# Grouping the count products of a graph kernel's sweep into runs of two and of four

## The chip, the core and the metric

The kernel runs on one core of one Trainium2 chip. Five engines of that core matter here, each working through its own list of instructions in order: TensorE (PE, matrix products; its weight loads are listed as PEld), VectorE (DVE), ScalarE (ACT), GpSimd (POOL, which here issues indirect DMAs) and SyncE (SP, which issues plain DMAs). Products are written to PSUM, eight banks of 2 KB for each of the 128 partitions; ACT and DVE read them there.

The metric is the device time of one launch in microseconds (us), lower is better. Three runs of the kernel before gave 1506.61 us as their median (1501.49 to 1509.82).

## What is computed

A graph layer over 6250 nodes with 200000 edges and 256 features, followed by a mixture of 64 experts and two normalisations. The edges come sorted by destination, and destinations crowd at low node numbers.

```python
deg_out = clip(segment_sum(ones, src), 1); deg_in = clip(segment_sum(ones, dst), 1)
h  = x * rsqrt(deg_out)[:, None]
m  = segment_sum(h[src], dst) * rsqrt(deg_in)[:, None]
x1 = m @ W_gc + b_gc + x @ W_res + b_res
core = top-2 of 64 experts on x1 (256 -> 512, gelu, -> 256)
y  = batch_norm(x1 + core) * gamma + beta
out = layer_norm(x + y)
```

The change concerns `segment_sum(h[src], dst)`, which the kernel does in a stage called the sweep.

## The kernel before, in words

The kernel first counts degrees, scales the rows and writes them to DRAM (`h_dram`) while keeping a copy in SBUF (`hrow`). Then comes the sweep, from about 171 to 906 us of the profile, and after it the routing, the experts and the normalisations.

**Two ways through the edges.** Edges are taken in groups of 128. The first 1118 groups, whose destinations lie close together, are *dense*: they are cut into 30 chunks (`DENSE`, numbered 0 to 29). A chunk covers a window of 128 destination nodes and consists of n parts; a part consists of k groups whose destinations fit into w columns. Chunks 0 to 4 have k = 4, 3, 2, 2, 2; from chunk 5 on k is 1, and (w, n) go from (4, 51) in chunk 5, (5, 50), (5, 46), (5, 42) in chunks 6 to 8 and (6, 39) to (6, 33) in chunks 9 to 12, over (7, 31) to (7, 27) in chunks 13 to 17 and (8, 26) to (8, 22) in chunks 18 to 23, to (9, 22) to (9, 20) in chunks 24 to 29. The remaining 445 groups are *gathered*: POOL fetches their source rows by an indirect DMA (L626) into a ring of eight tiles, and PE adds them to one PSUM bank `pg` (L631 and L632), 28 windows one after another.

**What one dense part costs.** `count` (L704) makes one product for each group, from two one-hot matrices in bf16, `lo` (128 source places) and `hotk` (49 source tiles times w columns): L712, 49·w columns wide, into a PSUM bank `pc`. So a product of chunk 14 is 343 columns wide. There are five banks `pc`. After the last group of a part ACT copies all but the first column of every source tile into the tile `counts` (L732, L729), and DVE adds the first column to what is there (L749). Both read the bank, so it comes free when both are done. The addition of part j isn't issued with part j: `carried(1)` (L745) leaves one part waiting at each call, so it is issued on DVE at the place of part j + 2.

**What makes the one-hots.** DVE makes `hotk` (L699) in cuts that hold two groups from w = 5 to w = 9, with four buffers: after the last product of a cut, the cut four further is issued, which waits on DVE until that product has read the buffer. `lo` (L287) is made once in eight groups. DVE also makes the one-hots `hot` of the gathered groups (L935, four groups at a time).

**What is multiplied.** `multiply(c, t)` (L755) multiplies the counts of chunk c by source tile t: two products of 258 and 256 columns in fp32r (L758, L759), t running over the 49 tiles of `hrow`. The sums of a chunk lie in one of two banks `sm`.

**What sets the order.** The generator `dense` (L879) writes the order out by hand, and all engines' lists follow it. For chunk c it walks over t = 0 to 48; ahead of `multiply(c, t)` it puts the parts of chunk c + 1 that fall on t, part j on t = 1 + 42·j // n. So the parts of one chunk are spread over the first 42 steps of the chunk before. Each item carries a weight in us, and a loop behind puts a gathered group between two items whenever the weights so far have passed the next group's due time. From t = 10 on, `x_step` (L853) puts in small steps that finish rows of an earlier window: on DVE L788, L792, L795, then L823, L828, L832, L835 and L836; on ACT a square root (L789) and a copy (L808); on PE transposes and gate products (L805, L814). When a gathered window is complete, PE adds an overlap product (L956), ACT copies `pg` out (L958), and the next window's first product waits for that copy, since there is one bank `pg`.

In the steps below, "chunk c" in connection with a time is the stretch in which chunk c is multiplied and chunk c + 1 is counted.

Of the kernel before, what the change touches and what calls it, by code (L numbers as in the profile page):

```python
# [161 lines left out]
def gnn_moe_kernel(ctx, tc, x_in, x_cols, src, dst, bases, nexts, firsts, parts, lasts, W_gc, b_gc, W_res, b_res, Wg, bg, w1, b1, w2, b2,  # L162
# [84 lines left out]
    with tc.tile_pool(name="edges", bufs=1) as ep, ExitStack() as later:  # L247
# [52 lines left out]
        with tc.tile_pool(name="late", bufs=1) as lp, tc.tile_pool(name="both", bufs=2) as bp, \  # L300
# [62 lines left out]
            for k, values in enumerate((LOW, HIGH)):  # L363
                c = 0
# [141 lines left out]
            for i in range(NGR // CG):  # L506
# [32 lines left out]
                for c in range(CG):  # L539
                    r = c % 2  # L540
# [19 lines left out]
                if i % 6 == 0 and 6 <= i <= 42:  # L560
                    r = i // 6 * 7
# [44 lines left out]
        with tc.tile_pool(name="xs", bufs=1) as xs, tc.tile_pool(name="hotg", bufs=2) as hg, \  # L606
# [12 lines left out]
            for i in range(NR):  # L619
                r = rp.tile([128, 2 * D + 2], F32R, name=f"r{i}")  # L620
# [29 lines left out]
            def halves(t):  # L650
                at = range(t - 1, min(t + 1, NS))
                for u in at:
                    S.activation(hrow[:, u, :D], f32(hrow[:, u, D:2 * D]), AF.Copy, scale=s_out[:, u:u + 1])
                for u in at:
                    V.scalar_tensor_tensor(hrow[:, u, D:2 * D], f32(hrow[:, u, D:2 * D]), s_out[:, u:u + 1],
                                           f32(hrow[:, u, :D]), op0=ALU.mult, op1=ALU.subtract)
                if t % 5 == 4 or t % 10 == 5:
                    n = 6 if t % 10 == 5 else 4
                    n -= max(t + 1 - NS, 0)
                    t0 = at[-1] + 1 - n  # L660
                    source_out(f32(hrow[:, t0:t0 + n, :2 * D]), h_dram, t0, n)
# [22 lines left out]
            def lo_of(q):  # L684

                if q * PAIRS < GD:
                    los[q] = hc.tile([128, PAIRS // 2, 128, 2], BF16, name="lo")
                    hot_pairs(los[q], lo_b, q * PAIRS, PAIRS, 128)

            def hot_of(q):  # L690

                if q >= len(cuts):
                    return
                a, b, w = cuts[q]
                e, m = a - a % 2, NS * w
                n = b + b % 2 - e
                hot = hc.tile([128, n * m], BF16, name="hotk", bufs=KB, padded_shape=[128, NS * LANES])
                hot = hot.rearrange("p (c j r) -> p c j r", j=m, r=2)
                V.tensor_tensor(hot, pairs(key, e, n, m), iota_h[:, None, :m, :].to_broadcast([128, n // 2, m, 2]),  # L699
                                ALU.is_equal)  # L700
                for g in range(a, b):
                    hots[g] = hot[:, (g - e) // 2, :, (g - e) % 2]

            def count(g):  # L704

                c, j, i = groups[g]
                g0, k, w, n = DENSE[c]
                if i == 0:
                    live["pc"] = ps_c.tile([128, 512], F32, name="pc")
                r = g % PAIRS  # L710
                pc = live["pc"][:, :NS * w]
                T.matmul(pc, los[g // PAIRS][:, r // 2, :, r % 2], hots.pop(g), start=(i == 0),  # L712
                         stop=(i == k - 1))
                if i == k - 1:
                    if j % 8 == 0:
                        _, live["at"] = nc.values_load_multi_w_load_instructions(
                            places[c:c + 1, j:j + 8], engines=(ACT_E, DVE_E), min_val=0, max_val=WIN - w,
                            skip_runtime_bounds_check_because="clipped to what the window leaves")
                    carried(1)
                    at, pc = live["at"][j % 8], pc.rearrange("p (t w) -> p t w", w=w)  # L720
                    if j == 0:
                        live["adds"], live["carry"], live["puts"] = [], [], []
                    if c == 0 and j == 0:
                        live["puts"].append(S.copy(counts[0][:, :, :w], pc).ins)
                    else:
                        if j == 0:
                            step = nc.values_load(step_i[0:1, c:c + 1], engines=(DVE_E,), min_val=0, max_val=WIN - 1,
                                                  skip_runtime_bounds_check_because="clipped to the window")
                            put = S.copy(counts[c % 2][:, :, 1:w], pc[:, :, 1:])  # L729
                            to, had = counts[c % 2][:, :, 0:1], counts[(c - 1) % 2][:, :, ds(step, 1)]  # L730
                        else:
                            put = S.copy(counts[c % 2][:, :, 1:][:, :, ds(at, w - 1)], pc[:, :, 1:])  # L732
                            to = had = counts[c % 2][:, :, ds(at, 1)]
                        for a in live["adds"]:
                            tc.declare_no_dep(put.ins, a, reason="other columns of the window")
                        live["carry"].append((to, pc[:, :, 0:1], had, j))
                        live["puts"].append(put.ins)
                if g % PAIRS == 1:
                    lo_of(g // PAIRS + 1)
                if g == cuts[cut_of[g]][1] - 1:  # L740
                    hot_of(cut_of[g] + KB)
                if i == k - 1 and j == n - 1:
                    carried(0)

            def carried(but):  # L745

                while len(live["carry"]) > but:
                    to, more, had, j = live["carry"].pop(0)
                    add = V.tensor_tensor(to, more, f32(had), ALU.add).ins  # L749
                    tc.add_manual_dep(add, live["puts"][j].name, SYNCED, reason="its bank, and the column of the part in front")  # L750
                    for a in live["puts"][j + 1:]:
                        tc.declare_no_dep(add, a, reason="columns behind it")
                    live["adds"].append(add)
# [125 lines left out]
            def dense():  # L879

                def of_one_hots(c):
                    g0, k, w, n = DENSE[c]
                    return n * (0.18 + k * (0.09 + 0.035 * w)) + 4.0

                lo_of(0)
                made_of = 1
                for q in range(KB):
                    hot_of(q)
                    halves(made_of)
                    made_of += 2  # L890
                S.activation(counts[0][:, 40:, :], iota_f[:, None, :].to_broadcast([128, NS - 40, WIN]), AF.Copy, scale=0.0)
                g, n = 0, DENSE[0][1] * DENSE[0][3]
                for g in range(n):
                    yield of_one_hots(0) / n, lambda g=g: count(g)
                    if g % 4 == 3:
                        yield 1.0, lambda t=made_of: halves(t)
                        made_of += 2
                for c in range(ND):
                    todo, us = {}, 0.0
                    if c < ND - 1:  # L900
                        g0, k, w, n = DENSE[c + 1]
                        us = max(0.021 + 0.0208 * w, (of_one_hots(c + 1) - 12.6) / (n * k),
                                 (n * (0.2 + w * 0.03) + 5.0 - 12.6) / (n * k))
                        for j in range(n):
                            todo.setdefault(1 + j * 42 // n, []).extend(range(g0 + j * k, g0 + j * k + k))
                    for t in range(NS):
                        for g in todo.get(t, []):
                            yield us, lambda g=g: count(g)
                        if c == 0 and t % 2 == 0 and made_of <= NS:
                            yield 1.0, lambda t=made_of: halves(t)  # L910
                            made_of += 2
                            if made_of > NS:
                                yield 0.0, lambda: first_rows()
                        if c == 0 and t == 45:
                            yield 0.0, lambda: left_edges()
                        yield 0.24, lambda c=c, t=t: multiply(c, t)
                        if 10 <= t < 46:
                            yield 0.04, lambda c=c, t=t: x_step(c, t)
# [44 lines left out]
            def first_rows():  # L963
                for n in range(NR):
                    fetch(ring[n], srcg[:, rows[n][1] - GD:rows[n][1] - GD + 1])
                hot_rows(0)

            now, n = 0.0, 0
# [155 lines left out]
    with tc.tile_pool(name="xw", bufs=1) as xw, tc.tile_pool(name="xl", bufs=3) as xl, \  # L1124
# [42 lines left out]
        with tc.manual_schedule():  # L1167
            sums = {}
            for t0 in range(ta, tb, 2):
                n = min(2, tb - t0)  # L1170
# [9 lines left out]
            for t0, z in sums.items():  # L1180
                n = min(2, tb - t0)
# [27 lines left out]
            for a, b in ((0, ta), (tb, NT)):  # L1209
                for t0 in range(a, b, 10):  # L1210
                    n = min(10, b - t0)
# [673 lines left out]
```

## Time and profile before

| | |
|---|---|
| median of three runs | 1506.61 us |
| the profiled execution | 1507.11 us |
| its span, first to last instruction | 1505.1 us |
| busy PE, DVE, ACT, POOL over the span | 90%, 75%, 51%, 53% |
| count products L712 | 1118, mean 304 ns |
| multiply products L758, L759 | 1470 each, mean 346 and 282 ns |
| copies out of `pc`, L732 | 879, mean 406 ns |
| additions of the first column, L749 | 908, mean 241 ns |
| one-hots L699 | 488, mean 507 ns |

A product's listed duration overlaps that of its neighbours, so the cost of one is read from the distance between starts. In rows of the timeline the columns are: start in us from the span's start, duration in us, engine, line, operation, what is written from what, shape, how many rows were merged (x2 is two instructions), and in brackets the idle time of the engine before it and what ended it.

### The profile page before, as it was taken

To read this page: it belongs to the slowest core of one execution; us is meant where nothing else is said; L and a number is where in the kernel's file an instruction comes from. 1 tells how busy PE (TensorE), PEld (TensorE's weight loads), DVE (VectorE), ACT (ScalarE), POOL (GpSimd) and SP (SyncE) were. 2 spreads that over 40 slices of the span, in tenths; PEclk is the share of its full clock that TensorE was granted. 3 is DMA by queue.
4 is the path that set the end of the run, shared out by engine and by line. 5 is a ranking of instruction groups with operands and counts; after the bars stand their busy time and mean duration, and the time that the engine had idled before them with its cause. 6 is when DMAs were issued, how large, how long until landed. Compare 5 with 4: busy or idle time off the path is not lost. (4 is left out here: it accounts for less than half of the span.)

```text
span 1505.1 us, 33098 instructions
## 1 busy us (share of the span) xinstructions
PE 1347.8 (90%) x9805; PEld 1127.7 (75%) x9805; DVE 1127.2 (75%) x3325; ACT 763.2 (51%) x1966; POOL 797.9 (53%) x897
## 2 busy tenths in 40 slices
PE   5999478988999999999999994699999999999783
PEld 3555266877888899999999993588788888788441
DVE  8999889988888888888777746745555655444587
ACT  4676544456666666665555533433343333333358
POOL 6000215777776677776666635256666667565100
PEclk8999789999999999999999996899999999999888
DMA  5899665778777778787777755669777788687645
GB/s 180 264 283 323 240 241 155 197 220 236 201 221 221 220 214 232 210 221 211 222 203 217 214 156 192 125 196 295 229 247 253 253 251 268 206 250 246 236 142 155
DMA packets 211234, 332.81 MB, mean 221 GB/s; under 512 B 27989, under 2 KB 142814, under 8 KB 211045
## 3 DMA queue, kind: packets, MB, share of 16 engines
q1 hardware_dynamic: 156035, 176.48, 37.5%
q0 software_dynamic: 47888, 146.88, 34.4%
q10 hardware_dynamic: 7122, 7.26, 1.7%
q8 instruction: 79, 1.29, 0.4%
q14 instruction: 110, 0.90, 0.2%
HBM read 250.92 MB, written 73.15 MB: 215 GB/s over the span
## 5 line engine op out<-in xcount | busy, mean ns | idle before, releaser
L626 POOL DMA_INDIRECT r<-h_dram,srcg x445 | 469.8, 1056 | 243.3 <-PE pc L712 80.2
L758 PE MATMUL sm<-hrow,counts 128*128 128x258 f32 x1470 | 487.0, 346 | 8.8 <-DVE counts L749 8.7
L732 ACT CAST counts<-pc 128x196 f32 (+7 forms) x879 | 356.9, 406 | 211.1 <-PE pc L712 175.4
L759 PE MATMUL sm<-hrow,counts 128*128 128x256 f32 x1470 | 394.5, 282 | 0.0
L712 PE MATMUL pc<-hotk,lo 128*128 128x245 bf16 (+7 forms) x1118 | 304.7, 304 | 42.5 <-DVE counts L749 20.3
L758 PEld LDWEIGHTS sm<-hrow,counts 128*128 128x128 f32 x1470 | 286.6, 195 | 27.4 <-issue 12.4
L699 DVE TENSOR_TENSOR hotk<-key,iota_h 128x784 bf16<-128x784 f16 (+4 forms) x488 | 247.6, 507 | 57.9 <-PE pc L712 55.8
L759 PEld LDWEIGHTS sm<-hrow,counts 128*128 128x128 f32 x1470 | 279.8, 190 | 1.3
L749 DVE TENSOR_TENSOR counts<-pc,counts 128x49 f32 x908 | 218.6, 241 | 48.3 <-ACT counts L732 10.3
L1523 ACT ACTIVATE hT<-ph,bc 128x112 f32<-128x112 f32 (+16 forms) x256 | 108.4, 428 | 265.4 <-PE ph L1521 255.1
L1521 PE MATMUL ph<-xgT,w1s 128*128 128x112 f32 (+17 forms) x1024 | 198.7, 340 | 0.4 <-DVE xgT L1506 0.4
L1521 PEld LDWEIGHTS ph<-xgT,w1s 128*128 128x128 f32 x1024 | 166.0, 192 | 20.5 <-issue 2.2
L1481 POOL DMA_INDIRECT y_dram<-ys,dest x124 | 120.7, 973 | 106.5 <-ACT ys L1575 68.9
L712 PEld LDWEIGHTS <-lo 128*128 128x128 bf16 x1118 | 99.5, 100 | 74.9 <-issue 17.1
L631 PE MATMUL pg<-r,hot 128*128 128x258 f32 x445 | 144.5, 325 | 2.9 <-DMA r<-h_dram,srcg 2.4
L1481 POOL DMA_INDIRECT xg<-x_dram,ids x124 | 119.0, 959 | 49.8 <-issue 15.2
L632 PE MATMUL pg<-r,hot 128*128 128x256 f32 x445 | 125.1, 281 | 0.0
L1537 PE MATMUL py<-w2s,hT 128*128 128x256 f32 (+4 forms) x440 | 105.2, 382 | 0.0
L470 PE MATMUL pr<-wcat,f 128*128 128x512 f32 x196 | 100.8, 638 | 0.8 <-DMA wcat<-in_L_gnn_W_res_dram 0.8
L1506 DVE TENSOR_SCALAR xgT<-pte,bsum 128x112 f32<-128x112 f32 (+14 forms) x128 | 48.7, 421 | 67.2 <-PE pte L1503 67.0
L287 DVE TENSOR_TENSOR lo<-lo_b,iota 128x1024 bf16<-128x1024 bf16 x140 | 96.0, 686 | 3.3 <-issue 2.9
L1559 PE MATMUL ph<-hT,w2s 128*128 128x208 f32 (+8 forms) x464 | 95.0, 358 | 0.0
(361 smaller groups left out, 1965.8 us busy)
## 6 DMA issues: line engine op xcount, KB each, us to landing
w1s<-in_L_gnn_w_dram SPq DMA_DIRECT2D x64, 512.0 KB
w2s<-in_L_gnn_w_dram SPq DMA_DIRECT2D x64, 512.0 KB
y_dram<-zeros SPq DMA_DIRECT2D x48, 256.0 KB
yr<-y_dram SPq DMA_DIRECT2D x10, 1024.0 KB
h_dram<-hrow SPq DMA_DIRECT2D x5, 1536.0 KB
r<-h_dram,srcg POOLq DMA_INDIRECT x445
f<-in_x_cols_dram SPq DMA_DIRECT2D x25, 256.0 KB
z_dram<-zeros ACTq DMA_DIRECT2D x7, 903.0 KB
```

The costliest lines, as they stand in the source:

```text
L626: G.indirect_dma_start(out=f32(r[:, :2 * D]), out_offset=None, in_=h_dram[:, :], in_offset=bass.IndirectOffsetOnAxis(ap=idx, axis=0))
L631: T.matmul(pg, hot, r[:, D:], start=first, stop=False)
L632: T.matmul(pg[:, :D], hot, r[:, :D], start=False, stop=last)
L699: V.tensor_tensor(hot, pairs(key, e, n, m), iota_h[:, None, :m, :].to_broadcast([128, n // 2, m, 2]), ALU.is_equal)
L712: T.matmul(pc, los[g // PAIRS][:, r // 2, :, r % 2], hots.pop(g), start=(i == 0), stop=(i == k - 1))
L732: put = S.copy(counts[c % 2][:, :, 1:][:, :, ds(at, w - 1)], pc[:, :, 1:])
L749: add = V.tensor_tensor(to, more, f32(had), ALU.add).ins
L758: T.matmul(sm, by, hrow[:, t, D:], start=(t == 0), stop=False)
L759: T.matmul(sm[:, :D], by, hrow[:, t, :D], start=False, stop=(t == NS - 1))
L1481: w = G.indirect_dma_start(**kw)
L1521: T.matmul(ph[:, :m], w1s[:, kk, c * 128:(c + 1) * 128], xgT[:, kk, :m], start=(kk == 0), stop=(kk == 1))
L1523: S.activation(hT[:, c, :m], ph[:, :m], AF.Gelu, bias=b1_e[:, c:c + 1])
```

## The change

From now on the unit that is put ahead of `multiply(c, t)` is not a group but all that falls on t, as one item; and where a part has one group (chunk 5 and later), parts are moved to the step of the first of two (while chunks 4 to 11 are multiplied, so parts of chunks 5 to 12) or of the first of four (while chunks 12 to 28 are multiplied, parts of chunks 13 to 29). Since a gathered group is only put between items, none can stand inside such a run any more; this holds for chunks 1 to 4 too, whose parts otherwise stay where they are. The weights add up to the same sum.

```diff
                         us = max(0.021 + 0.0208 * w, (of_one_hots(c + 1) - 12.6) / (n * k),
                                  (n * (0.2 + w * 0.03) + 5.0 - 12.6) / (n * k))
+                        at_once = 1 if k > 1 else 2 if c < 12 else 4
                         for j in range(n):
-                            todo.setdefault(1 + j * 42 // n, []).extend(range(g0 + j * k, g0 + j * k + k))
+                            todo.setdefault(1 + (j - j % at_once) * 42 // n, []).append(range(g0 + j * k, g0 + j * k + k))
                     for t in range(NS):
-                        for g in todo.get(t, []):
-                            yield us, lambda g=g: count(g)
+                        if t in todo:
+                            yield us * sum(len(r) for r in todo[t]), lambda t=t, todo=todo: [count(g) for r in todo[t] for g in r]
```

What this does to PE's list, at the start of chunk 13 (parts 0 to 3 of chunk 14; weight loads left out). Before:

```order
L759 MATMUL sm1_2856<-hrow_104,counts1_2821 128x256
...
L712 MATMUL pc_10016<-hotk_9913,lo_9868 128x343
L758 MATMUL sm1_2856<-hrow_104,counts1_2821 128x258
...
L712 MATMUL pc_10042<-hotk_9913,lo_9868 128x343
L631 MATMUL pg_9753<-r6_2849,hot_9872 128x258
L632 MATMUL pg_9753<-r6_2849,hot_9872 128x256
...
L712 MATMUL pc_10052<-hotk_9932,lo_9868 128x343
```

With the change:

```order
L759 MATMUL sm1_2856<-hrow_104,counts1_2821 128x256
...
L712 MATMUL pc_10016<-hotk_9913,lo_9864 128x343
...
L712 MATMUL pc_10040<-hotk_9913,lo_9864 128x343
...
L712 MATMUL pc_10045<-hotk_9923,lo_9864 128x343
...
L712 MATMUL pc_10049<-hotk_9923,lo_9864 128x343
L631 MATMUL pg_9761<-r6_2849,hot_9874 128x258
L632 MATMUL pg_9761<-r6_2849,hot_9874 128x256
```

Four count products, each into another bank, now follow one another. Until the next four, five pairs of L758 and L759 and two pairs of L631 and L632 stand there. Over chunks 4 to 11 the count products stand in 167 runs where they stood in 314, and over chunks 12 to 28 in 108 where they stood in 411.

DVE's list in chunk 13, from the additions of parts 4 and 5 of chunk 14 to that of part 6 (sequencer rows left out). Before:

```order
L749 TENSOR_TENSOR counts0_2820<-pc_10071,counts0_2820 128x49
...
L749 TENSOR_TENSOR counts0_2820<-pc_10079,counts0_2820 128x49
L287 TENSOR_TENSOR lo_10102<-lo_b_94,iota_2_73 128x1024
L699 TENSOR_TENSOR hotk_10104<-key_92,iota_h_85 128x686
L788 TENSOR_SCALAR s_in_10108<-z_9779 125x2
...
L749 TENSOR_TENSOR counts0_2820<-pc_10092,counts0_2820 128x49
```

With the change:

```order
L749 TENSOR_TENSOR counts0_2820<-pc_10071,counts0_2820 128x49
...
L749 TENSOR_TENSOR counts0_2820<-pc_10075,counts0_2820 128x49
L287 TENSOR_TENSOR lo_10089<-lo_b_94,iota_2_73 128x1024
L699 TENSOR_TENSOR hotk_10091<-key_92,iota_h_85 128x686
L936 TENSOR_TENSOR hot_10095<-keyg_93,iota_f_71 128x512
L788 TENSOR_SCALAR s_in_10108<-z_9783 125x2
...
L749 TENSOR_TENSOR counts0_2820<-pc_10081,counts0_2820 128x49
```

On DVE nearly the same instructions stand in nearly the same order (here one `hot` has moved behind the two additions). What differs is where on PE's side they belong: the last row, the addition of part 6, is issued at the place of part 8, which is now the first of the third run of four; part 11, the last of that run, is the one that takes the bank of part 6.

## The prediction

> **What bounds the kernel now.** I first read the page's slices (PE, then DVE, 37.6 us each), to see which engine is full where.
>
> ```profile
> span 1505.1 us, 33098 instructions
> PE   5999478988999999999999994699999999999783
> DVE  8999889988888888888777746745555655444587
> ```
>
> The sweep is slices 5 to 24. Both engines are full at first, and DVE's share falls while PE's stays. The windows cut the sweep finer: length, then busy time of PE, weight loads, DVE, ACT and POOL with their instructions, PE's clock, DMA share and GB/s. The stretches are chunks 4 to 7, 8 to 12, 13 to 17, 18 to 23, and 24 to 28.
>
> ```profile
> 323.40:434.70 111.30, 101.65 (x779) 89.26 (x779) 98.33 (x362) 70.19 (x205) 83.03 (x80) 1.00 0.78 220
> 434.70:555.30 120.60, 115.64 (x896) 105.79 (x897) 104.29 (x372) 75.83 (x193) 85.52 (x80) 1.00 0.79 220
> 555.30:661.90 106.60, 106.18 (x828) 99.41 (x827) 89.51 (x304) 66.89 (x155) 78.55 (x73) 1.00 0.78 219
> 661.90:788.30 126.40, 126.40 (x975) 119.62 (x974) 101.27 (x337) 75.90 (x164) 82.36 (x81) 1.00 0.75 213
> 788.30:890.20 101.90, 101.90 (x778) 96.47 (x778) 73.78 (x234) 58.71 (x118) 65.25 (x64) 1.00 0.75 211
> ```
>
> From 555 us on PE never stops (106.18 of 106.60, then all): there a saved product is saved time, and a stalled one is lost. Up to 555 us PE is open for 10 and 5 us and DVE is busy 88% and 86%; the two hold each other up. What PE waits for there is in the view of the additions L749 between 323 and 555 us (who waited, us, times); in the same view of 555 to 890 us PE's count products don't appear.
>
> ```profile
>   PE pc L712: 10.4, 27
> ```
>
> So banks come free just in time before 555 us, and early enough after it.
>
> **What a run saves on PE.** The timeline of PE gives a count product alone (294 columns, then 196), and in a run of two and of four.
>
> ```profile
> 450.32 0.28 PE L759 MATMUL sm<-hrow,counts 128*128 128x256 f32 x1
> 450.44 0.30 PE L712 MATMUL pc<-hotk,lo 128*128 128x294 bf16 x1
> 450.48 0.39 PE L758 MATMUL sm<-hrow,counts 128*128 128x258 f32 x1
> 450.70 0.28 PE L759 MATMUL sm<-hrow,counts 128*128 128x256 f32 x1
> ...
> 309.97 0.28 PE L758 MATMUL sm<-hrow,counts 128*128 128x258 f32 x1
> 310.09 0.28 PE L759 MATMUL sm<-hrow,counts 128*128 128x256 f32 x1
> 310.21 0.44 PE L712 MATMUL pc<-hotk,lo 128*128 128x294 bf16 x2
> 310.38 0.38 PE L758 MATMUL sm<-hrow,counts 128*128 128x258 f32 x1
> 310.60 0.28 PE L759 MATMUL sm<-hrow,counts 128*128 128x256 f32 x1
> ...
> 330.78 0.28 PE L759 MATMUL sm<-hrow,counts 128*128 128x256 f32 x1
> 330.90 0.26 PE L712 MATMUL pc<-hotk,lo 128*128 128x196 bf16 x1
> 330.94 0.36 PE L758 MATMUL sm<-hrow,counts 128*128 128x258 f32 x1
> 331.14 0.28 PE L759 MATMUL sm<-hrow,counts 128*128 128x256 f32 x1
> ...
> 219.28 0.28 PE L759 MATMUL sm<-hrow,counts 128*128 128x256 f32 x1
> 219.40 0.52 PE L712 MATMUL pc<-hotk,lo 128*128 128x196 bf16 x4
> 219.70 0.37 PE L758 MATMUL sm<-hrow,counts 128*128 128x258 f32 x1
> 219.91 0.28 PE L759 MATMUL sm<-hrow,counts 128*128 128x256 f32 x1
> ```
>
> One fp32r product costs 0.12 us (309.97 to 310.09). From 450.32 to 450.70 lie two of them and one count product: 0.38 - 0.24 = 0.14 us for it. From 310.09 to 310.60 lie two and two: 0.51 - 0.24 = 0.27, so the second cost 0.13. A product that is taken into a run saves 0.01 us at 294 columns. At 196 columns it is 0.36 - 0.24 = 0.12 alone and 0.63 - 0.24 = 0.39 for four, 0.03 us saved for each of three. No run of 343 columns or more exists in this trace. I take 0.01 for all, since 294 is the nearer width, with 0 and 0.03 as ends. Runs fall from 314 to 167 over chunks 4 to 11 and from 411 to 108 over chunks 12 to 28: 147 · 0.01 = 1.5 us and 303 · 0.01 = 3.0 us, together -4.5 us (0 to -13.5).
>
> [...]
>
> **What a run costs in banks.** There are five banks `pc`. Part j + 5 takes the bank of part j, which needs the copy on ACT and the addition on DVE, and that addition is issued at the place of part j + 2. With single parts DVE may lag behind PE by three parts before PE stalls. In a run of four the addition of part 6 is issued at the first (part 8) and the bank is wanted by the last (part 11), three products later. At 343 columns a product in a run is about 0.157 us (estimate: 0.135 · 343/294), so the allowed lag shrinks to 0.47 us. How far DVE lags in the present kernel, at part 6 of chunk 14: PE starts part 8 and part 11, DVE makes the addition.
>
> ```profile
> 560.20 0.33 PE L712 MATMUL pc<-hotk,lo 128*128 128x343 bf16 x1
> ...
> 562.14 0.33 PE L712 MATMUL pc<-hotk,lo 128*128 128x343 bf16 x1
> ```
>
> ```profile
> 561.51 0.23 DVE L749 TENSOR_TENSOR counts<-pc,counts 128x49 f32 x1
> ```
>
> It ends at 561.74, 1.54 us after its place and 0.40 before its bank is wanted. With only 0.47 us of room it would have held PE for 1.07 us. That is the bad end. But between runs PE now spends longer on other products, and DVE has only additions and one-hots of the last run to do. So I walk one period, with DVE's costs as distances between starts and ACT's from a string of copies.
>
> ```profile
> 565.35 0.68 DVE L935 TENSOR_TENSOR hot<-keyg,iota_f 128x512 fp32r<-128x512 f16 x1
> 565.95 0.28 DVE L636 TENSOR_SCALAR overg<-iota_f,shift 128x128 f32<-128x128 f32 x1
> ...
> 566.30 0.68 DVE L287 TENSOR_TENSOR lo<-lo_b,iota 128x1024 bf16<-128x1024 bf16 x1
> 566.90 0.51 DVE L699 TENSOR_TENSOR hotk<-key,iota_h 128x686 bf16<-128x686 f16 x1
> 567.33 0.59 DVE L749 TENSOR_TENSOR counts<-pc,counts 128x49 f32 x2
> 567.82 0.51 DVE L699 TENSOR_TENSOR hotk<-key,iota_h 128x686 bf16<-128x686 f16 x1
> ```
>
> ```profile
> 561.63 0.20 ACT L789 ACTIVATE s_in<-s_in 125x2 f32<-125x2 f32 x1 [1.04 <-DVE s_in L788]
> 562.40 2.18 ACT L732 CAST counts<-pc 128x294 f32 x5 [0.56 <-PE sm L759]
> ```
>
> A `hot` costs 0.60, a `lo` 0.60, a `hotk` 0.43, two additions 0.49, a copy 0.44 us. Second run of chunk 13 in the changed order, T its first product. `hotk` must wait for the second product, which starts 0.157 in and takes 0.33: about T + 0.5, done T + 0.95. The additions of parts 4 and 5 need the copies, which begin once the first product is out (about T + 0.4) and end about T + 0.85 and T + 1.3, so they are done at T + 1.5. Then `lo` to T + 2.1, `hotk` to T + 2.5, `hot` to T + 3.1, L788 to T + 3.2, and the addition of part 6 ends at T + 3.4. PE's period is four products (0.63) and seven pairs (7 · 0.24 = 1.68), 2.3 us, and the last of the third run wants the bank at T + 2.3 + 0.47 = T + 2.8. PE stalls 0.6 to 0.7 us. The same walk over the other runs of that chunk gives 0.4 and 0.2 us, then nothing; 1.3 us. ACT adds to this where its square root stands ahead of the copies and waits for L788 (1.04 us above).
>
> From such walks I estimate 1.2, 1.3, 0.8, 0.6 and 0.3 us for chunks 12 to 16 (7 columns), together 4.2; about 0.4 us each for chunks 17 to 22, whose period is 2.9 us for hardly more DVE work, 2.4; and 0.3 for the rest. Sum +6.9 us; the ends are 0 and 23 us (a quarter of a microsecond at each of 91 runs that are not first in their chunk, a quarter of the 1.07 us).
>
> Named behind the stalled product on PE: every multiply and gathered product, since PE works in order; POOL's next fetch waits for them but has a ring of eight.
>
> A second, smaller wait is ACT's: where a gathered window closes just behind a run, its copy out of `pg` stands behind four copies (4 · 0.44 = 1.8 us), and the next gathered product is due 0.5 to 1.0 us of PE time after the overlap product. In the changed order this is so in chunks 13, 14, 18, 19 and 22. Some 0.3 us each, +1.5 us (0 to 4).
>
> In chunks 4 to 11 the second of two products comes a multiply (0.24 us) or more earlier than it did, while its bank comes when DVE gets there. If the 27 waits became 54 of 0.3 us more, it would be +8 us; if twos let DVE run more evenly, at most the 10.4 us go. I take +2, because DVE's work is the same and sets that stretch. Chunks 0 to 3 I leave at 0: only gathered products move, and DVE is full there.
>
> The Trainium skill (Perfetto Trace Analysis, section Optimizing Tensor Performance, Matmuls) asks that independent products rotate through banks so that the emptying of one overlaps the next's products. That speaks against a run that takes four of five banks at once. The trace's 10.4 us of bank waits before 555 us agree with it.
>
> **The sum.** -4.5 + 6.9 + 1.5 + 2 = +5.9 us. The profiled execution had 1507.1 us (2.0 of it outside the span), half a microsecond over the median, so 1513 us.
>
> **The rivals.**
>
> *PE gains and nothing waits.* For it: the view of one-hots L699 between 555 and 890 us shows DVE idle for PE's count products:
>
> ```profile
>   PE pc L712: 46.9, 74
> ```
>
> so DVE has room, 14% of 335 us, and might be ahead at each run's start. Against it is the lag of 1.54 us above, in a stretch where that room exists too. Then -4.5 us, 1502.6, or at 0.03 us a product -13.5, 1493.6. [...]
>
> *Every run waits.* The mechanism of the walk, at all 91 runs: from the point where DVE's lag at the start of a run passes 0.47 us as a rule, PE pays what DVE owes. +23 - 3 = +20, 1527. For it: the lag of part 6. Against: at 9 columns the period grows to some 3.4 us and DVE's work doesn't follow (73.78 of 101.90 busy).
>
> *The first stretch eases.* Twos make DVE's waits for ACT rarer and PE's bank waits before 555 us go: up to -10.4 there, against the +8.4 behind; about 1503. For it: DVE is idle 13 us in 323 to 434 while PE waits too. Against: no instruction of DVE gets cheaper.
>
> That the change doesn't do what it says is excluded by the listed rows: the runs stand in PE's list.
>
> **How the numbers follow.** Forecast as walked (1507 to 1519) 0.46; nothing waits 0.22; every run waits 0.19; the first stretch eases 0.13. About 0.5%, 7.5 us, is what a measurement can tell here: faster is under 1499.1, slower over 1514.1. Faster: half of the first rival, some of the third, 0.14. Slower: all of "every run waits" and nearly half of the forecast, 0.40. Within: 0.46. The range runs from 1498 to 1528, with the likeliest case's own 1507 to 1519 in it.
>
> **What would show it.** In the changed profile, the windows behind 555 us should show PE open for some us in chunks 12 to 16, ended by DVE's L749, and hardly any in chunks 23 to 28. Starts inside a run should be about 0.155, 0.175 and 0.20 us apart at 343, 392 and 441 columns. PE's waits for `pc` should lie on the last product of a run. The forecast is wrong if PE stays closed there, if starts in a run are as far apart as a product alone costs, or if the first stretch moves by more than 5 us.

## The result and the profile after

| | before | after |
|---|---|---|
| median, same chip | 1506.98 us (6 runs, 1501.49 to 1509.82) | 1520.64 us (6 runs, 1519.38 to 1524.48) |
| the profiled execution | 1507.11 us | 1520.51 us |
| its span | 1505.1 us | 1518.8 us |

After / before is 1.0095, with a 95% interval of 1.0078 to 1.0113: the change costs 13.7 us, where +5.9 was predicted. The range held it; the loss was more than twice the sum.

The page's slices of the kernel after show PE's slices 25 and 26 fuller, since the sweep ends later; the loss itself is too small to be seen in them.

```profile
span 1518.8 us, 33067 instructions
PE   5999488988999999999999995789999999999783
DVE  9999889988888887877777755845555655454597
```

The windows of the same five stretches as in the prediction (chunks 4 to 7, 8 to 12, 13 to 17, 18 to 23, 24 to 28; length, then busy time of PE, weight loads, DVE, ACT and POOL, PE's clock, DMA share and GB/s), each cut up to 2.4 us later than at the same events:

```profile
326.30:437.70 111.40, 100.51 (x781) 88.01 (x780) 98.50 (x364) 70.38 (x205) 82.30 (x79) 1.00 0.77 218
437.70:560.80 123.10, 116.37 (x900) 104.10 (x899) 105.36 (x376) 76.51 (x194) 86.30 (x81) 1.00 0.77 215
560.80:673.00 112.20, 105.37 (x819) 95.22 (x818) 89.69 (x298) 66.26 (x154) 71.62 (x73) 1.00 0.73 206
673.00:805.40 132.40, 127.90 (x978) 115.27 (x977) 104.17 (x339) 76.43 (x165) 82.87 (x81) 1.00 0.74 203
805.40:909.50 104.10, 102.39 (x786) 92.56 (x785) 73.12 (x231) 58.07 (x117) 63.93 (x63) 1.00 0.73 205
```

The first stretch is about as long as before (111.40 against 111.30 us). From 560.8 us on PE is open for 6.8, 4.5 and 1.7 us, where before it stood open for 0.4, 0 and 0. The clock was 1.00 in all of them, before and after.

For a finer account I cut at the copies of the finished sums (L762). Up to the end of chunk 3 the kernel is 1.8 us longer, chunks 4 to 11 are 0.4 longer (209.0 to 209.4), chunks 12 to 28 are 14.7 longer (358.4 to 373.1), and what lies behind, where no list changed, is 3.2 shorter; the sum is the 13.7 of the spans. I have no cause for the first and the last of these; the experiments below show that both vary by more from one execution to the next.

What PE waited for in chunks 12 to 28 (532 to 890 us before, 534 to 907 after), by the view of waits; the columns are who waited for what, us in total, times, and the longest. Before:

```profile
PE sm L758 <- DVE counts L749: 1.0, 2, 0.7
```

After:

```profile
PE pc L712 <- DVE counts L749: 10.6, 19, 1.1
PE pg L631 <- issue: 1.5, 1, 1.5
PE pg L631 <- ACT resg L959: 1.2, 3, 0.7
PE sm L758 <- DVE counts L749: 1.0, 1, 1.0
```

The count products wait for the additions of DVE, which before they never did here. This view counts from the listed end of the product in front, and that overlaps; by distances between starts (what is over 0.152, 0.173 and 0.198 us at 343, 392 and 441 columns) the loss is 14.8 us in 25 of 97 runs of four, all of it on the fourth product. The other waits of PE in the stretch come to 5.3 us by distances, and before there were 1.6 in all. So 20.1 - 1.6 = 18.5 us of waits came and the stretch grew by 14.7, which leaves about 3.8 us for what the runs saved.

In chunks 4 to 11 the same rows are, before and then after:

```profile
PE pc L712 <- DVE counts L749: 10.4, 27, 1.2
PE sm L758 <- DVE counts L749: 2.6, 6, 0.7
```

```profile
PE pc L712 <- DVE counts L749: 11.6, 27, 1.6
PE sm L758 <- DVE counts L749: 1.1, 4, 0.4
```

They moved between products and hardly changed in sum.

**One stall, read through.** Chunk 28 multiplies and chunk 29 is counted. The timeline of PE has the third run of four (parts 8 to 11):

```profile
892.72 0.28 PE L759 MATMUL sm<-hrow,counts 128*128 128x256 f32 x1
892.84 0.76 PE L712 MATMUL pc<-hotk,lo 128*128 128x441 bf16 x3
894.46 0.37 PE L712 MATMUL pc<-hotk,lo 128*128 128x441 bf16 x1 [0.86 <-DVE counts L749]
```

The x3 end at 893.60, the last of them began at 893.60 - 0.37 = 893.23, so the step inside the run is 0.39 / 2 = 0.195 us; the fourth should have begun at 893.43 and began at 894.46. It needs the bank of part 6. DVE between the additions of parts 4 and 5 and those of parts 6 and 7:

```profile
890.78 0.62 DVE L749 TENSOR_TENSOR counts<-pc,counts 128x49 f32 x2
891.31 0.69 DVE L287 TENSOR_TENSOR lo<-lo_b,iota 128x1024 bf16<-128x1024 bf16 x1
891.91 0.61 DVE L699 TENSOR_TENSOR hotk<-key,iota_h 128x882 bf16<-128x882 f16 x1
892.44 0.37 DVE L788 TENSOR_SCALAR s_in<-z 125x2 f32<-125x2 f32 x1
892.51 0.69 DVE L936 TENSOR_TENSOR hot<-keyg,iota_f 128x512 fp32r<-128x512 f16 x1
893.11 0.16 DVE L792 RECIPROCAL s_in<-s_in 125x2 f32<-125x2 f32 x1
893.30 0.88 DVE L795 SCALAR_TENSOR_TENSOR xr<-z,s_in,xr 125x256 f32<-125x256 f32 x2
894.16 0.52 DVE L749 TENSOR_TENSOR counts<-pc,counts 128x49 f32 x2
```

DVE works without a pause from 890.78 on. The copy of part 6, the third of four that ACT makes from 890.10 to 892.17, ended at about 891.65, so its addition is 2.5 us late. It is issued at the place of part 8, behind one-hots and the four steps that finish rows of an earlier window (L788, L792 and two L795; I call them the row steps). PE's period between the two runs (889.64 to 892.84, 3.2 us) is no longer than that list (890.78 to 894.16, 3.4 us).

The row steps run once in a stretch, from t = 10 on, and only in 15 of the 17 chunks 12 to 28, since chunks 16 and 24 have no rows to finish. In all 15 the third run of four stalls on its last product (part 11: 15 stalls, 10.8 of the 14.8 us); in chunks 16 and 24 it doesn't. Two more things stand at that place. L792 needs the square root that ACT makes of what L788 wrote, and now often nothing lies between them on DVE. The view of the line L792 in chunks 12 to 28 has this wait, and before it had none:

```profile
  ACT s_in L789: 3.0, 10
```

And at parts 0, 8, 16 and 24 the next eight column numbers are loaded into registers of ACT and DVE (L716), ahead of the addition that is issued there. The view of that line has the load on DVE's sequencer (min, median, max in ns), and the timeline of DVE at part 8 of chunk 16 has 0.66 us of standing ahead of the addition of part 6, most of it while that load runs (it starts at 612.7 and takes 0.62 us):

```profile
L716 DVEq TENSOR_LOAD <-places x58: 602/612/1653, 534.9 to 901.5; - x58
...
612.22 0.16 DVE L788 TENSOR_SCALAR s_in<-z 125x2 f32<-125x2 f32 x1
612.66 0.17 DVE L792 RECIPROCAL s_in<-s_in 125x2 f32<-125x2 f32 x1 [0.27 <-ACT s_in L789]
613.49 0.52 DVE L749 TENSOR_TENSOR counts<-pc,counts 128x49 f32 x2 [0.66 <-DVE s_in L792]
```

So there are three suspects for part 11: the shorter lag by itself, the row steps with their wait for ACT, and the load.

### The profile page after: what moved, and what is told of

It is laid out like the page before. It is cut to its first block, busy times and chain, and to the rows that moved or that the text cites. A ratio compares the mean times of both kernels' runs of the same rounds, so it can differ in the third digit from the quotient of the medians.

```text
span 1518.8 us, 33067 instructions
## 1 busy us (share of the span) xinstructions
PE 1346.0 (89%) x9805; PEld 1112.0 (73%) x9805; DVE 1134.9 (75%) x3325; ACT 763.1 (50%) x1966; POOL 794.2 (52%) x897
## 5 line engine op out<-in xcount | busy, mean ns | idle before, releaser
L626 POOL DMA_INDIRECT r<-h_dram,srcg x445 | 464.7, 1044 | 266.1 <-PE pg L632 133.1
L758 PE MATMUL sm<-hrow,counts 128*128 128x258 f32 x1470 | 414.6, 307 | 6.6 <-DVE counts L749 6.3
L759 PE MATMUL sm<-hrow,counts 128*128 128x256 f32 x1470 | 380.8, 283 | 0.0
L758 PEld LDWEIGHTS sm<-hrow,counts 128*128 128x128 f32 x1470 | 281.1, 191 | 25.9 <-issue 11.8
L712 PE MATMUL pc<-hotk,lo 128*128 128x245 bf16 (+7 forms) x1118 | 236.4, 300 | 56.6 <-DVE counts L749 33.3
L759 PEld LDWEIGHTS sm<-hrow,counts 128*128 128x128 f32 x1470 | 281.4, 191 | 0.8
L749 DVE TENSOR_TENSOR counts<-pc,counts 128x49 f32 x908 | 219.5, 242 | 61.9 <-ACT counts L732 15.3
L631 PE MATMUL pg<-r,hot 128*128 128x258 f32 x445 | 146.9, 330 | 7.3 <-DMA r<-h_dram,srcg 3.4
L712 PEld LDWEIGHTS <-lo 128*128 128x128 bf16 x1118 | 79.6, 101 | 83.8 <-issue 19.5
L632 PE MATMUL pg<-r,hot 128*128 128x256 f32 x445 | 125.8, 283 | 0.0
L631 PEld LDWEIGHTS pg<-r,hot 128*128 128x128 f32 x445 | 84.2, 189 | 33.8 <-issue 19.0
```

Of the source, the lines that this page charges most:

```text
L626: G.indirect_dma_start(out=f32(r[:, :2 * D]), out_offset=None, in_=h_dram[:, :], in_offset=bass.IndirectOffsetOnAxis(ap=idx, axis=0))
L631: T.matmul(pg, hot, r[:, D:], start=first, stop=False)
L632: T.matmul(pg[:, :D], hot, r[:, :D], start=False, stop=last)
L758: T.matmul(sm, by, hrow[:, t, D:], start=(t == 0), stop=False)
L759: T.matmul(sm[:, :D], by, hrow[:, t, :D], start=False, stop=(t == NS - 1))
```

## The experiments

The kernels below ran on three other chips than the result, on which the kernel before takes 1603.8 to 1607.0 us (e_singles, e_before_again and e_spread on the second of them, e_load on the third, the others on the first); each ratio is against the kernel before on the same chip, and lengths of stretches are compared among those chips only. "Twos" and "fours" are runs; the table's lengths are of the profiled executions. Singles took 374.3 to 376.1 us in chunks 12 to 28 in three of them, so differences of 2 us there are not read. Waits by distances are taken as on the first chip.

| label | chunks 4 to 11 / 12 to 28 counted in | ratio, 95% interval | us in chunks 4 to 11 | in 12 to 28 |
|---|---|---|---|---|
| e_before_again | singles / singles (the kernel before) | 0.9984 [0.9963, 1.0005] | 224.3 | 374.3 |
| e_singles | singles / singles, unit changed | 0.9996 [0.9977, 1.0015] | 226.4 | 375.9 |
| e_early_only | twos / singles | 1.0024 [1.0000, 1.0049] | 228.0 | 376.1 |
| e_late2 | singles / twos | 1.0010 [0.9987, 1.0032] | 226.6 | 374.7 |
| e_late3 | twos / threes | 1.0039 [1.0011, 1.0067] | 228.5 | 378.6 |
| e_late_only | singles / fours | 1.0110 [1.0073, 1.0146] | 224.5 | 387.6 |
| e_again | twos / fours (the change) | 1.0095 [1.0074, 1.0116] | 229.5 | 386.0 |
| e_soon | twos / fours, additions issued sooner | 1.0157 [1.0122, 1.0192] | 229.0 | 390.6 |
| e_spread | twos / fours, row steps set apart | 1.0106 [1.0080, 1.0132] | 227.2 | 393.2 |
| e_load | twos / fours, addition ahead of the load | 1.0113 [1.0082, 1.0144] | 226.8 | 390.7 |
| e_before_nox | singles / singles, no row steps | | 223.4 | 374.9 |
| e_nox | twos / fours, no row steps | | 225.3 | 379.5 |

**Which part costs.** The change does three things: it makes what falls on one step one item, it counts in twos early, and it counts in fours late. Each alone, on the one line that sets the length of a run:

```diff
-                        at_once = 1 if k > 1 else 2 if c < 12 else 4
+                        at_once = 1                                    # e_singles
+                        at_once = 1 if k > 1 else 2 if c < 12 else 1   # e_early_only
+                        at_once = 1 if k > 1 else 1 if c < 12 else 4   # e_late_only
+                        at_once = 1 if k > 1 else 2 if c < 12 else 3   # e_late3
+                        at_once = 1 if k > 1 else 1 if c < 12 else 2   # e_late2
```

> Only the change of the unit: every part stays at its own step, but what falls on one step is one item, so that no gathered product stands between count products of one step (it matters for chunks 1 to 4 and little behind). Theory 'the cost is bunching': 0.999 to 1.002. Rival 'keeping gathered products out costs by itself' (the 2.4 us by which chunks 0 to 3 are longer with the change): 1.0015 to 1.004, with chunks 0 to 3 two us or more longer than in the run below.

> Twos for chunks 5 to 12 alone; chunks 13 to 29 one part at a time, as before. Theory 'late addition': the twos cost or save almost nothing, chunks 4 to 11 take 209 to 212 us and PE has no waits behind them: 1505 to 1510 us. Rival 'the twos lose too': 1511 or more.

> Fours for chunks 13 to 29 alone; chunks 5 to 12 one part at a time (gathered products still stay between items). Theory 'late addition': all of the loss sits in the fours, 1517 to 1521 us, and chunks 4 to 11 take about 209 us as before the change. Rival 'the twos lose too': 3 us or more under the changed kernel.

> Twos as in the change for chunks 5 to 12, but threes instead of fours for chunks 13 to 29 (142 runs instead of 108). With five banks the third product of a run takes the bank of a part whose addition was issued at the last place of the run before. Theory 'late addition': the waits on the last product nearly vanish (under 3 us), 269 products are saved about 0.01 us each, 2.7 us, so the sweep's second part is about as long as before or 2 us shorter: 1504 to 1510 us. Rival 'DVE short of time': some 10 us of the loss stay, 1515 or more. Rival 'runs are slow by themselves': three quarters of the loss stay, about 1516.

> Single parts while chunks 4 to 11 are multiplied, twos from chunk 12 on. Theory 'lag': the bank of part j is wanted two products after the place of its addition at worst plus a whole period before it, so hardly a wait; 200 products save 0.01 us each; with nothing lost in chunks 4 to 11 the ratio is 0.997 to 1.002. Rival 'any bunching costs': half of what fours cost, 1.004 to 1.007.

> The change once more, beside the runs below on one chip. On the first chip it took 1.0095 of the time before, with 14.8 us of waits on the last product of a run of four over chunks 12 to 28. Either theory expects 1.006 to 1.013 here and the waits within 3 us of that; it is the measure for the other three.

> The kernel before, once more, for its stretches on the chip of these runs. Any theory: a ratio of 0.997 to 1.003, and waits of PE for counting banks in chunks 12 to 28 of 5 us or less.

The unit alone costs nothing (0.9996), twos early at most half a per cent, and fours late 1.1%, as much as the whole change (1.0095 beside it). Between runs of three and of four lie 386.0 - 378.6 = 7.4 us in chunks 12 to 28; twos cost nothing there, and gain nothing that can be measured (374.7 against the 376.1 of singles on the same chip). So the loss isn't proportional to the bunching: most of it comes with the fourth product. That is the lag by which DVE may be late: with fours the wanted bank is that of the part whose addition is issued at the head of the same run. In the view of waits, chunks 12 to 28, the run of the change has

```profile
PE pc L712 <- DVE counts L749: 13.6, 17, 1.6
```

and the runs of twos, in the view of the line L712,

```profile
  DVE counts L749: 2.2, 4
```

No version here beats the kernel before.

Some of these forecasts were missed. The waits on fourth products in e_again are 23.1 us by distances, where 14.8, give or take 3, was expected. On these chips PE has waits without runs as well, some 17 us in chunks 12 to 28 of e_before_again where the first chip had 1.6 (an estimate from the same distances), so not every wait in a run is a loss, and the lengths decide. Threes wait 6.0 us on third products, where under 3 was forecast, and their 1.0039 lies between that forecast (1510 us would be 1.002) and the rivals (1515 us would be 1.005). Twos early, 1.0024, stand between the theory and its rival. In e_singles chunks 0 to 3 end 3.6 us later than in e_before_again (344.0 and 340.4), as the rival wanted, but in e_late2, with the same lists there, they end at 338.1: single executions differ that much, and the ratio of 0.9996 decides.

**Is it the late issue of the addition?** In e_soon each addition is issued one part sooner from chunk 13 on, so that the addition of part 6 stands in the run of part 7.

```diff
                         live["puts"].append(put.ins)
+                        if c > 12:
+                            carried(1)
```

> The changed kernel with the same runs of two and four on PE, but for chunks 13 to 29 the addition of part j is issued at the place of part j+1 instead of j+2, so that the additions of parts 5 and 6 stand with the run before and part 11's bank is asked for a whole period later. Theory 'late addition' (the last product of a run waits for a bank whose addition is issued only at the run's first): the waits on the fourth product fall from about 15 us to under 4, PE's saving stays, 1505 to 1511 us. Rival 'DVE short of time' (DVE has too much to do in a period, whatever the place of the addition): the waits move to other rows and the time stays over 1516. Rival 'runs are slow by themselves' (copies of four banks by ACT set the pace): time unchanged, about 1520.

It got slower: 1.0157 and 390.6 us, as the rival 'DVE short of time' had it. The waits on fourth products fell to 3.8 us by distances, as the theory wanted, but 6.6 us now lie on second and third products, and DVE stood in its list waiting for the copy that it was to follow. What DVE waited for ahead of the additions in chunks 12 to 28, with the change (e_again) and then in e_soon:

```profile
  issue: 10.1, 24
  ACT counts L732: 6.8, 26
```

```profile
  ACT counts L732: 29.8, 49
  issue: 27.3, 47
```

It waited 23 us more for the copies, and 17 us more where the trace has no releaser ("issue"). Inside runs PE's waits fell by 14 us against e_again; its other waits, on gathered products, transposes and multiply products, rose by some 17 us. The longest rows of e_soon's view of waits in these chunks (its two added lines shift the numbers: L807 is L805, L797 is L795, L760 is L758, L751 is L749):

```profile
PE pg L631 <- issue: 5.9, 3, 3.4
PE sm L807 <- DVE xr L797: 3.8, 4, 1.4
PE sm L760 <- DVE counts L751: 3.4, 2, 1.9
```

The second and third row are DVE being late; for the first that is not shown. The profiled execution took 1612.6 us against a median of 1625.1, so this profile doesn't show where all of the loss lies. The copies of a run of four end one after another on ACT, the last 2.5 us after the run's first product (889.64 to 892.17 in the stall above), and DVE waits in order for whichever it meets too soon. So with fours both places that were tried are bad.

**Is it the row steps?** First without them:

```diff
-                    live["steps"] = x_make(z, xr, 2, node_rows(x_rows, t0, 2))
+                    live["steps"] = [lambda: None] * 3 + [lambda: node_dma(nc.sync, False, xr[:, :2, :], node_rows(x_rows, t0, 2))]
```

> The change, with the steps L788, L789, L792 and L795 (the scaling of an earlier window's rows) left out of the sweep; the loads and the store of those rows stay, so the rows are stored unscaled. Theory 'DVE's other work stands ahead': those steps lie between the additions of parts 5 and 6 and make the third run of each chunk late, so the waits on fourth products fall from about 15 us to 5 or less, and the time against its own twin (before, with the same steps left out) to 1.000 to 1.004. Rival 'the shorter lag alone': the runs of four leave too little room whatever stands on DVE; 10 us or more of the waits stay and the ratio to the twin is 1.007 or more.

> The kernel before, with the same steps left out: the twin of the run above. PE is closed from chunk 12 on, so nothing moves there; in chunks 4 to 11, where DVE and PE hold each other up, about 1.7 us of DVE work a chunk goes, so 0 to 13 us are saved: 0.991 to 1.000 of the time before under both theories.

The rows are stored unscaled, and what lies behind the sweep, fed with them, takes 10.8 ms in both, so only the sweep is compared. In the twin the sweep hardly moved, as forecast (374.9 us in chunks 12 to 28). The waits for additions in chunks 12 to 28 fell to less than a third of the 13.6 us above:

```profile
PE pc L712 <- DVE counts L749: 4.0, 7, 1.3
```

By distances part 11 went from 16.8 us in 15 stalls to 6.2 in 7, and fours cost 379.5 - 374.9 = 4.6 us in these chunks where with the row steps they cost 386.0 - 376.1 = 9.9 (e_again less e_early_only, same chip). So the row steps carry about half of the loss; the rest stays without them. Of the waits on fourth products 12.9 of 23.1 us stay, where the theory gave 5 at most and the rival 10 at least; 6 of the 12.9 have no releaser in the trace ("issue"). The 4.6 us are 0.3% of the kernel's time, within the 0.4% of the theory and under the rival's 0.7%. Each got half.

Then with the row steps whole but set apart, behind t = 3, 6, 10 and 17 in place of 10, 12, 14 and 16:

```diff
-                if u == 0 and "x" in live:
+                if twice and t < 10:
+                    return
+                if (u == 0 if twice else t == 3) and "x" in live:
...
-                if u in (0, 2, 4, 6) and live.get("steps"):
+                if (u in (0, 2, 4, 6) if twice else t in (3, 6, 10, 17)) and live.get("steps"):
...
-                if u == 10:
+                if u == (10 if twice else 11):
...
-                        if 10 <= t < 46:
-                            yield 0.04, lambda c=c, t=t: x_step(c, t)
+                        if 2 <= t < 46:
+                            yield 0.04 if t >= 10 else 0.0, lambda c=c, t=t: x_step(c, t)
```

> The change, with the steps L788, L792 and the two L795 of an earlier window's rows kept whole but set wider apart: behind t = 3, 6, 10 and 17 in place of 10, 12, 14 and 16 (and their transposes one step later), so that at most one L795 stands between two runs of four, but for the last two chunks. Theory 'DVE's other work stands ahead of the addition': the waits on part 11 fall from 11 us to 5 or less, the stretch of chunks 12 to 28 is 3 to 7 us shorter than with the change, and the ratio to before is 1.004 to 1.007. Rival 'what counts is DVE's share of work, wherever it stands': the waits only move to other parts, and the ratio stays at 1.008 to 1.011.

Half of the stalls went where the steps went. By distances part 11 fell from 16.8 us in 15 stalls (e_again) to 8.3 in 9, not to the 5 of the theory; part 7, which had 2.2 us, now has 7.7 us in 9 stalls. The whole is no better (1.0106), and chunks 12 to 28 took 393.2 us where less than e_again's 386.0 was forecast. The rival's number came true. The largest stall that stays on part 11 is 2.65 us in chunk 13: there the addition of part 6 (607.89) still stands behind L792 and one L795 (606.89 to 607.56), and then waits 0.33 us for its copy. How one on part 7 came about, in chunk 25 of e_spread, DVE and then PE:

```profile
878.23 0.69 DVE L938 TENSOR_TENSOR hot<-keyg,iota_f 128x512 fp32r<-128x512 f16 x1
878.83 0.28 DVE L636 TENSOR_SCALAR overg<-iota_f,shift 128x128 f32<-128x128 f32 x1
879.03 0.17 DVE L788 TENSOR_SCALAR s_in<-z 125x2 f32<-125x2 f32 x1
879.46 0.17 DVE L792 RECIPROCAL s_in<-s_in 125x2 f32<-125x2 f32 x1 [0.27 <-ACT s_in L789]
879.59 0.24 DVE L749 TENSOR_TENSOR counts<-pc,counts 128x49 f32 x1
```

```profile
879.89 0.37 PE L712 MATMUL pc<-hotk,lo 128*128 128x441 bf16 x1 [1.16 <-DVE counts L749]
```

The reciprocal waits for the square root on ACT, and the addition of part 2 waits behind it, and behind `hot` and `overg` (0.8 us from 878.23 to 879.03). So it isn't these steps at that place alone: in this stall other work of DVE in the period, and its wait for ACT, came out at the next fourth product. The new place put the wait for ACT into a period that had been free of it; a spread without that was not tried.

**Is it the load?** The addition is issued ahead of it:

```diff
                 if i == k - 1:
+                    carried(1)
                     if j % 8 == 0:
                         _, live["at"] = nc.values_load_multi_w_load_instructions(
...
-                    carried(1)
```

> The change, with the addition of part j - 2 issued ahead of, and not behind, the load of the next eight column numbers into registers of ACT and DVE (L716, 0.61 us on DVE's sequencer, at parts 0, 8, 16 and 24, so at the head of the third run of four). Theory 'the load of column numbers': in the changed kernel DVE stands still for 0.34 to 0.70 us ahead of the addition of part 6 in nine of the fifteen stalls on part 11, together 5 us; these go, part 11 falls from 11 us to about 6, and the ratio to before is 1.005 to 1.008. Rival 'the row steps alone': those stalls are DVE's work and its wait for the square root; part 11 stays at 9 us or more and the ratio at 1.008 to 1.011.

By distances part 11 fell from 16.8 us in 15 stalls (e_again, on another chip) to 10.6 in 12. That is about the drop that the theory gave, but the level is the rival's (9 us or more). Part 15 rose from 2.8 to 4.5 us and part 7 from 2.2 to 3.5, and the whole took 1.0113, no less than the change and nearest to the rival. The view of waits in chunks 12 to 28 still has

```profile
PE pc L712 <- DVE counts L749: 7.9, 13, 1.4
...
PE pc L712 <- DVE xr L795: 3.2, 3, 1.3
```

So stalls moved to other parts here too. The load is a part of the stalls where they show, but issuing the addition ahead of it did not take the loss away.

**What stands after this.** Bunching by four costs about 1%, by three 0.4% together with the early twos, and by two late nothing that can be measured. In the stalls read through, PE pays where DVE's list between two runs is longer than PE's; the row steps are about half of the loss. For the other half the runs name no single culprit: moving the row steps, the additions or the load moved the stalls and left the sum or raised it.

## Why the prediction was right, and where it was off

- **PE closed behind 555 us, so that a stall there is lost time.** Right: with 18.5 us of new waits the stretch grew by 14.7, and the 3.8 us between the two are a saving that the next point finds in another way.
- **A product in a run saves 0.01 us.** Right. From one L759 to the next the median is 0.239 us with no count product between, 0.405 with one of 343 columns (kernel before) and 0.558 with a run of two (e_late2): 0.166 us alone, 0.319 for two, so 0.013 saved. At 441 columns 0.449 and 0.643 give 0.016. For the 303 products over chunks 12 to 28 0.013 us make 3.9, where 3.0 stood in the sum. The steps to the third and fourth product of a run are 0.152, 0.173 and 0.198 us, where 0.155, 0.175 and 0.20 were forecast. The Trainium skill (TensorE: Matmul & The Clock Gate, Back-to-back issue gap) gives columns / 2.4 plus 2.5 ns as the gap of an isolated product, by estimate 0.186 us at 441 columns; the 0.195 us above are longer.
- **Stalls on the last product of a run, released by L749.** Right, and on no other product of the run. The walk of chunk 13 gave 0.6 to 0.7, 0.4 and 0.2 us for the third to fifth runs; measured are 0.69, 1.04 and nothing over 0.1.
- **"About 0.4 us each for chunks 17 to 22 ... and 0.3 for the rest."** This is the step that failed. The sum's 4.2 + 2.4 + 0.3 = 6.9 us were 6.5 + 5.0 + 3.3 = 14.8. I walked the period of chunk 13, in which only L788 stands ahead of the addition of part 6, and let the stalls shrink with the columns, since PE's period grows "for hardly more DVE work". But with wider and so fewer parts the third run moves from t = 12 to t = 17 and so behind more and more of the row steps, in chunk 28 behind all four. My periods had of them only L788, neither the two L795 (0.86 us from 893.30 to 894.16) nor L792's wait for ACT, and not the load of registers. The windows that I quoted, 73.78 of 101.90 us busy, are a mean over a stretch; what decides is the fullest period in it. Leaving the row steps out took away about half of the loss of fours; the sign that chunks 23 to 28 would hardly wait failed with this term.
- **ACT's copy of `pg` behind four copies, +1.5.** The waits of gathered products were 3.3 us by distances, 1.6 of it released by L959 and one of 1.7 that has no releaser in the trace.
- **Chunks 4 to 11, +2.** 0.4 us: the waits moved from one product to the next. On the slower chips twos took 226.8 to 229.5 us there and singles 224.3 to 226.6, by the means 2.7 us more.
- **The rivals.** "Nothing waits" and "the first stretch eases" did not come. "Every run waits" was nearer in time (1527 against 1513, measured 1520.6) but not in kind: 25 of 97 runs waited, most of them the third of their chunk. For "the first stretch eases" the terms -4.5, -10.4 and +8.4 would have made 1500.6 and not 1503.

The Trainium skill's page Perfetto Trace Analysis (Optimizing Tensor Performance, Matmuls) asks for banks that rotate, so that emptying overlaps computing. The banks did rotate before and after. Here the trace adds that what counted was the distance in the order of work from the instruction that frees a bank to the product that takes it.

## What to carry to other kernels

When work is bunched, count for each buffer how much of the waiting engine's time lies between the place at which its release is issued and the product that takes it, and compare it with the fullest period of the releasing engine, all its occasional work included, not with its mean share. Occasional steps, a few to a stretch, weigh there; moving them moved the stalls, and issuing the release sooner made its engine wait for what the release needs. Shorter runs cost little or nothing (threes and twos here), but the saving was 0.01 us a product, so there was little to win.

## What was unexpected

Three of the four chips were 6.4 to 6.6% slower with the same kernel (1603.8 to 1607.0 against 1507.0 us), at nearly the same granted clock (0.950 against 0.959 in the mean). The window of the experts' stage in the kernel before, on the first chip and on a slower one:

```profile
979.00:1397.50 418.50, 409.18 (x2296) 354.26 (x2297) 222.64 (x769) 150.70 (x376) 262.75 (x254) 1.00 0.77 242
```

```profile
1026.90:1491.60 464.70, 425.11 (x2295) 359.82 (x2296) 217.92 (x769) 148.96 (x376) 261.20 (x254) 0.98 0.69 218
```

DVE, ACT and POOL are busy for about the same time (within 2.2%), and the stage is 46 us longer. In the sweep waits appear for which the trace has no releaser ("issue"), on all engines; for the count products, over the whole kernel on the slower chip:

```profile
PE pc L712 <- issue: 16.9, 37, 1.3
```

On the first chip this row doesn't appear. What these stalls are stays open. They are why lengths of stretches are not compared between the first chip and the others, and why small differences among the experiments are not read: with the same lists the changed kernels ended chunk 3 at 338.1 to 345.1 us, and took 650.7 to 663.0 us behind chunk 28.
